# A second stream of forward transforms in a scan kernel, and later stores and loads around it

## The chip, the cores and the metric

The kernel runs on one core of one Trainium2 chip. The metric is the device time of one execution in microseconds (us); the time before is the median of three runs. Everything is computed in fp32.

## What is computed

Two layers, on an input of 4 images of 128 channels, 128 x 128 points each.

The first layer is a state-space scan. Each image is a sequence of 16384 tokens. Two small matrix products with a ReLU, then a projection to 256 channels of `x_in` and 256 of `z`; a causal convolution of 4 taps and a SiLU make `u`. From `u` come `delta` (softplus) and, per token, 16-vectors B and C. For each of the 256 channels and 16 states

```
h = h * exp(delta * A) + delta * B * u        # scan over the tokens
y = sum over states of h * C                  # plus u * D, times silu(z)
```

A projection back to 128 channels, a group norm over the image, a SiLU and the residual follow; the result is called x1.

The second layer filters x1 in the frequency domain. Four weights for each image come from a softmax over pooled, normed and projected channels. With X the two-dimensional real Fourier transform of x1 and four fixed filters, the product reduces to X times X times the weighted sum of the filters; it is transformed back, and half of x1 is added.

## The kernel before

**First block (`block0`).** It goes over 128 chunks of 512 tokens, 32 chunks an image, one image after the other. A chunk is cut into 16 slots, a slot being two scans of 128 partitions (32 channels by 4 states) by 512 tokens. All work is put into lists `todo[slot, phase]`, and a loop at the end of `block0` issues slot after slot, and in a slot phase after phase, in an order written out by hand:

```
for phase in ("turn", "sums", "pe", "exps", "late", "act", "pool", "dbu", "early", "gate", "scans", "dve", "end"):
```

A phase is a place in this order and not an engine. So each engine's queue has a fixed order, and what it waits for it gets from semaphores.

What a slot needs: ACT makes the decays (`da`, L469, `exps`). The products of delta, u and B come from POOL (`dbu`, L439) for three of each four scans; for the fourth PE transposes a tile `bt` (`dbu_turn`, L459) into the PSUM bank `b0`, of which there is one. DVE scans (L488). The product with C is made by DVE (L490) for some scans and by POOL (L495) for the others, and ACT keeps the last column as the next chunk's start (L491, L636). PE adds up the states in the bank `y` (`sums`, L505 for the term with D, L509), and DVE gates the result (`gate`, L519). A chunk has two halves of channels, and `y` has one bank: the sums of the second half, from slot 11 on, wait for the gate of the first half in slot 10.

Beside this, `pre(k)` prepares chunk k while chunk k-1 is scanned. `du_pool` (L340) multiplies delta by u on POOL, `du_turn(h)` (L320) transposes half of it on PE into a bank `pt`, and `bt_act` (L336) copies it on ACT, scaled, into the tile `bt`, eight pieces for each half. Before, the pieces of the first half stand in slots 8 to 11, `du_turn(1)` in slot 12 and the pieces of the second half in slots 12 to 14, in every chunk.

While image b+1 is scanned, image b is finished (`finish`): its group norm is applied in the chunks for which `norming(k)` holds (the third to the eighteenth of each later image; load L710 and L711, SiLU on ACT, addition on DVE, store of x1), and then come aggregation products (`agg`) for the pooling. From the 53rd chunk on, one stream of forward transforms is woven in (`spectrum`): three, three or two channels of x1 a chunk are loaded (slot 4), transformed over the height (slot 12, `over_h` L559, copied by ACT at L563) and over the width (slot 13, `over_w` L573, copied by ACT at L577), and stored to DRAM as `spec`. Three such pieces make a group of 8 channels. With EARLY = 2 the groups of image 0 and nine of image 1 are transformed there: 25 of 64.

**Second block (`block1`).** It goes over 64 units; a unit is 8 channels of one image, in three steps of 3, 3 and 2 channels. A unit whose spectrum is ready loads it (`sx`); the others transform x1 on PE (`over_h` L955 into `pa`, copied to `sa`; `over_w` L974 into `px`). All then take squares and products (ACT, DVE), sums (POOL), and the transform back (PE L1012, L1013, L1024; DVE L1018, and L1031 for the residual), and store `out`. The filters of a group are weighted on ACT (L922) and added on POOL (L932). Filter tiles `ft` come by DMA and serve several units. Image 3 is finished in the first units, its norm in steps 9 to 57 (two chunks in three steps, added by DVE at L724) and its aggregation after that, in steps 70 to 102, one chunk a step. So image 3 comes last; the images of the units, in order, with e where the spectrum is ready and F where it is made here, are, before:

```
0e 2F 1F  x7   0e 2F 1e  x6   3F 3F 3F
0e 3F 2F 3F 1e 3F 3F   0e 3F 2F 3F 1e 3F 3F   0e 3F 2F 3F 1e 3F 3F 3F
```

Units are counted from 0. All loads and stores of both blocks are issued on SP's queue, in the order of the program.

Of the kernel before, what the change touches and what calls it, by code (L numbers as in the profile page):

```python
# [26 lines left out]
F32 = mybir.dt.float32  # L27
# [7 lines left out]
T = 512  # L35
DG = 32
SQ = 4
NP = 16
CC = 8
EARLY = 2  # L40
KEEP = 4
LAG = 7
EPS = 1e-5
# [125 lines left out]
def block0(tc, s):  # L169
# [4 lines left out]
    with ExitStack() as ctx:  # L174
# [27 lines left out]
        def pre(k):  # L202
# [167 lines left out]
            if k == 0:  # L370
# [20 lines left out]
                    (NP, "pe", z_mm), (NP, "act", z_act), (NP + 3, "act", z_silu),  # L391
                ]
            late = k == 1
            return [
                (-14 - 10 * late, "pe", load), (-7 - 13 * late, "pe", h1_mm), (-6 - 13 * late, "act", h1_act),
                (-5 - 6 * late, "pe", xm_mm), (-4 - 6 * late, "act", xm_act),
# [7 lines left out]
                (9, "act", partial(bt_act, 0, 1, 3)),  # L404
                (10, "act", partial(bt_act, 0, 3, 5)), (11, "act", partial(bt_act, 0, 5, 8)),
                (12, "pe", partial(du_turn, 1)), (12, "act", partial(bt_act, 1, 0, 3)),
                (13, "act", partial(bt_act, 1, 3, 6)), (14, "act", partial(bt_act, 1, 6, 8)),
                (16, "pe", partial(rep_load, 1)),
            ]

# [102 lines left out]
        def post(k):  # L513

            b, i = divmod(k, NCH)
            d = st[k]

            def gate(j):
                nc.vector.tensor_mul(d["zs"][:, j, :], d["zs"][:, j, :], d["y", j])  # L519
# [22 lines left out]
            return [  # L542
                (26, "dve", partial(gate, 0)), (34, "dve", partial(gate, 1)), (36, "pe", o_mm), (37, "act", o_act),
                (49, "act", o_square),
                (50, "dve", done),
            ]

        def spectrum(b, c0, n):

            g = {}  # L550

            def load():
                g["x"] = p1.tile([s.H, 3, s.W], F32, tag="fx", name=f"fx_{b}_{c0}")
                nc.sync.dma_start(out=g["x"][:, 0:n], in_=s.x1[b][c0 : c0 + n].rearrange("c h w -> h c w"))

            def over_h():
                g["pa"] = psp.tile([s.W, 3, 2 * s.WF], F32, tag="pp", name=f"pp_fa_{b}_{c0}")
                for q in range(n):
                    nc.tensor.matmul(g["pa"][:, q], g["x"][:, q], s.fh, start=True, stop=True)  # L559

            def evict():
                g["sa"] = p1.tile([s.W, 3, 2 * s.WF], F32, tag="fs", name=f"fs_{b}_{c0}")
                nc.scalar.copy(g["sa"][:, 0:n], g["pa"][:, 0:n])  # L563

            def over_w():
                half = s.H // 2
                g["px"] = psp.tile([s.H, 3, 2 * s.WF], F32, tag="pp", name=f"pp_fx_{b}_{c0}")
                for q in range(n):
                    re, im = g["sa"][:, q, 0 : s.WF], g["sa"][:, q, s.WF :]
                    for (data, a, b_), start in (((re, s.fwr, s.fwr), True), ((im, s.fwi, s.fwm), False)):  # L570
                        for at, w in ((0, a), (1, b_)):
                            o = g["px"][at * half : (at + 1) * half, q]
                            nc.tensor.matmul(o, data[:, at : at + half], w, start=start, stop=not start)  # L573

            def store():
                x = p1.tile([s.H, 3, 2, s.WF], F32, tag="fq", name=f"fq_{b}_{c0}")
                nc.scalar.copy(x[:, 0:n].rearrange("h c r k -> h c (r k)"), g["px"][:, 0:n])  # L577
                nc.sync.dma_start(out=s.spec[b][:, c0 : c0 + n], in_=x[:, 0:n])

            return [  # L580
                (4, "pe", load), (12, "pe", over_h), (12, "end", evict), (13, "pe", over_w), (13, "end", store),
            ]
# [27 lines left out]
        chunk = NCH + NCH // 2 + 4  # L610
        for b in range(EARLY):
            for c0 in reversed(range(0, C, CC)):
                chunk = max(chunk, (b + 1) * NCH + NCH // 2 + 4)
                if chunk + 3 > n_chunks:
                    break
                for at, n in ((0, 3), (3, 3), (6, 2)):
                    for slot, phase, f in spectrum(b, c0 + at, n):
                        todo[slot + chunk * NP, phase].append(f)
                    chunk += 1
# [12 lines left out]
        with tc.manual_schedule():  # L632
            for n in range(min(slots), max(slots) + 1):
                for phase in ("turn", "sums", "pe", "exps", "late", "act", "pool", "dbu", "early", "gate", "scans", "dve", "end"):
                    for f in todo[n, phase]:
                        f()  # L636

# [52 lines left out]
def finish(s, io, b, first, norm, agg, add="dve", sums=True):  # L690
# [27 lines left out]
    def norm_dve(i):  # L718
        o, n = g["o", i], g.pop(("n", i))
        if sums:  # L720
            total = g["stat"][:, 0, i : i + 1]
            nc.vector.tensor_tensor_reduce(o, n, g["x", i], 1.0, 0.0, ALU.add, ALU.add, total)
        else:
            nc.vector.tensor_add(o, n, g.pop(("x", i)))  # L724
        nc.sync.dma_start(out=s.x1flat[b][:, i * T : (i + 1) * T], in_=o)

    def norm_stats(i):
        o = g.pop(("o", i))
# [84 lines left out]
def block1(tc, s):  # L813
# [10 lines left out]
    with ExitStack() as ctx:  # L824
# [76 lines left out]
        def load(n):  # L901
            if n < N:
# [124 lines left out]
        def residual(e, n, m, k):  # L1027
            if m == 0:
                u[n].ot = p2.tile([H, CC, W], F32, tag="ot", name=f"ot_{n}")
            o, xt = u[n].ot[:, m : m + k], u[n].xt[:, m : m + k]  # L1030
            nc.vector.scalar_tensor_tensor(o, xt, s.resw[0:H], e.po[:, 0:k], ALU.mult, ALU.add)  # L1031
            if m + k == CC:
                c0, b = units[n]
                nc.sync.dma_start(out=s.out[b, :, c0 : c0 + CC], in_=u[n].ot)

        with tc.manual_schedule():
            load(0)
            load(1)
            for t in range(3 * N + LAG + 3):
# [114 lines left out]
```

## Time and profile before

| | us |
|---|---|
| median of 3 runs | 7047.36 (7046.41 to 7050.6) |
| the profiled execution, its own time | 7042.62 |
| its span | 7040.8 |
| DVE busy | 6840.5 (97%) |
| POOL busy | 6802.5 (97%) |
| ACT busy | 6167.2 (88%) |
| PE busy | 5615.9 (80%) |

The span is the time from the first instruction to the last, as the profiler saw it. An engine's busy time is the sum of its instructions; the share of the whole span is a mean over stages with different limits, so the windows by stage say more. "Granted clock" is the share of its full speed at which PE was let run. A wait is named by the engine that ended it.

### The profile page before, as it was taken

How to read it: one execution, taken by the hardware profiler on the slowest of the kernel's cores; microseconds unless marked ns; L12 is line 12 of the kernel's file. 1: busy time of each engine (PE TensorE's matmuls, PEld its weight loads, DVE VectorE, ACT ScalarE, POOL GpSimd, SP SyncE). 2: the span in 40 equal slices, each digit the busy share in tenths (PEclk: the TensorE clock that was granted, in tenths of full speed). 3: DMA queues.
4: the chain of work that ended last, by engine and by line, in shares of the span. 5: the costliest groups of instructions: out<-in, count | busy, mean ns of one | idle time of the engine just before them, and what ended most of it. 6: DMA issues, size and time to landing. Idle time of an engine off the chain costs nothing. (4 is left out here: it accounts for less than half of the span.)

```text
span 7040.8 us, 95517 instructions
## 1 busy us (share of the span) xinstructions
PE 5615.9 (80%) x28742; PEld 2685.4 (38%) x28742; DVE 6840.5 (97%) x7914; ACT 6167.2 (88%) x13839; POOL 6802.5 (97%) x3010
## 2 busy tenths in 40 slices
PE   7777777777777788888777787887777787878999
PEld 3333333333333333333333333333333333327888
DVE  8999999999999999999999999999999999998877
ACT  7888888888888888889999988899999999888886
POOL 8999999999999999999999999999999999998887
PEclk9999989988998989999999999999999999999999
DMA  6676666766777777777877777777777877767865
GB/s 157 150 164 159 153 162 154 164 158 163 194 182 187 191 168 175 175 181 170 200 191 193 197 173 177 175 183 170 198 193 190 203 173 178 169 174 281 271 218 191
DMA packets 758088, 1285.91 MB, mean 183 GB/s; under 512 B 81584, under 2 KB 192704, under 8 KB 757568
## 3 DMA queue, kind: packets, MB, share of 16 engines
q1 hardware_dynamic: 757280, 1279.27, 73.2%
q8 instruction: 226, 3.70, 0.2%
q14 instruction: 294, 2.41, 0.1%
q10 hardware_dynamic: 288, 0.52, 0.0%
HBM read 1023.43 MB, written 256.06 MB: 182 GB/s over the span
## 5 line engine op out<-in xcount | busy, mean ns | idle before, releaser
L439 POOL TENSOR_TENSOR hb<-rdu,rB 128x512 f32<-128x512 f32 (+2 forms) x1537 | 3614.3, 2370 | 62.4 <-ACT rdu L360 32.9
L469 ACT ACTIVATE da<-rdelta,amat 128x512 f32<-128x512 f32 x4096 | 2804.4, 703 | 103.2 <-DVE h L488 98.7
L488 DVE TENSOR_TENSOR_SCAN da<-da,st,hb 128x512 f32<-128x512 f32 x2000 | 2446.9, 1266 | 25.3 <-ACT da L469 24.7
L495 POOL TENSOR_TENSOR hb<-h,rC 128x1024 f32<-128x1024 f32 (+1 forms) x1048 | 2411.9, 2303 | 55.0 <-DVE h L488 45.0
L490 DVE TENSOR_TENSOR hb<-da,rC 128x512 f32<-128x512 f32 x2064 | 1308.8, 673 | 2.2
L488 DVE TENSOR_TENSOR_SCAN h<-da,st,b 128x512 f32<-128x512 f32 x992 | 1257.6, 1268 | 2.7 <-PE b L459 2.7
L509 PE MATMUL y<-hb,sel 128*32 128x512 f32 x8192 | 1233.6, 675 | 12.9 <-POOL hb L495 12.5
L488 DVE TENSOR_TENSOR_SCAN h<-da,st,hb 128x512 f32<-128x512 f32 x976 | 1222.6, 1255 | 2.8 <-POOL hb L495 2.1
L459 PE MATMUL b<-ident,bt 128*128 128x128 f32 x4096 | 712.7, 295 | 487.2 <-DVE h L488 426.0
L255 PE MATMUL pp_cv<-xm,wck 128*128 128x512 f32 x2048 | 989.4, 627 | 3.0 <-ACT zs L249 2.6
L336 ACT ACTIVATE bt<-dut,xdt 128x256 f32<-128x256 f32 x2040 | 845.3, 483 | 114.7 <-PE dut L320 113.6
L459 PEld LDWEIGHTS b<-ident,bt 128*128 128x128 f32 x4096 | 516.3, 149 | 948.8 <-DVE h L488 708.3
L491 ACT COPY st<-da 128x1 f32<-128x1 f32 x2064 | 288.1, 163 | 454.6 <-DVE hb L490 450.5
L255 PEld LDWEIGHTS pp_cv<-xm,wck 128*128 128x128 f32 x2048 | 387.9, 199 | 632.5 <-issue 456.7
L320 PE MATMUL dut<-ident,du 128*128 128x128 f32 x1024 | 199.0, 328 | 475.4 <-POOL du L340 450.3
L932 POOL TENSOR_TENSOR wb<-wb,term 128x1040 f32<-128x1040 f32 x166 | 398.9, 2404 | 52.5 <-ACT term L922 47.0
L505 PE MATMUL y<-u,diag 128*128 128x512 f32 x512 | 307.1, 684 | 166.2 <-DVE zs L519 165.4
L320 PEld LDWEIGHTS dut<-ident,du 128*128 128x128 f32 x1024 | 141.9, 165 | 651.6 <-POOL du L340 582.0
L469 ACT ACT_TABLE_LOAD x261 | 334.9, 1283 | 4.6
L509 PEld LDWEIGHTS y<-hb,sel 128*32 128x32 f32 x8192 | 169.8, 113 | 374.5 <-issue 241.3
L294 PE MATMUL pp_dt<-xd,wdt 128*128 128x256 f32 x1024 | 286.8, 405 | 25.7 <-ACT xd L275 8.8
L244 PE MATMUL pp_z<-xm,win 128*128 128x512 f32 x512 | 274.8, 634 | 39.0 <-ACT fq L577 37.0
(197 smaller groups left out, 8376.9 us busy)
## 6 DMA issues: line engine op xcount, KB each, us to landing
rdelta<-dd SPq DMA_DIRECT2D x1020, 256.0 KB, 4.9
rdu<-dd SPq DMA_DIRECT2D x1020, 256.0 KB, 7.9
rC<-bc SPq DMA_DIRECT2D x512, 256.0 KB, 7.1
rB<-bc SPq DMA_DIRECT2D x512, 192.0 KB, 4.4
dd<-delta SPq DMA_DIRECT2D x255, 256.0 KB, 7.6
dd<-du SPq DMA_DIRECT2D x127, 512.0 KB, 6.6
ft<-in_filt_w SPq DMA_DIRECT2D x108, 520.0 KB, 6.4
xr<-in_x SPq DMA_DIRECT2D x128, 256.0 KB, 2.8
```

What stands on the lines that cost most here:

```text
L255: nc.tensor.matmul(ps["cv", j], w, d["xm"][:, t : t + T], start=t == 0, stop=t == KC - 1)
L320: nc.tensor.transpose(ps["dut", h][:, 2 * t + j, :], d["du"][:, j, at : at + P], s.ident)
L336: nc.scalar.activation(o, src, AF.Copy, scale=scale)
L439: nc.gpsimd.tensor_tensor(hb[:, p : p + n, :], d["du", j][:, m : m + n, :], d["B"][:, p - 1 : p - 1 + n, :], ALU.mult)
L459: nc.tensor.transpose(b[:, t * P : (t + 1) * P], src, s.ident)
L469: nc.scalar.activation(da, d["delta", j][:, m, :], AF.Exp, scale=s.amat[:, c : c + 1])
L488: nc.vector.tensor_tensor_scan(o, das[q], b, init, ALU.mult, ALU.add)
L490: nc.vector.tensor_tensor(hb[:, p + q, :], das[q], d["C"][:, p + q, :], ALU.mult)
L495: nc.gpsimd.tensor_tensor(hb[:, ps, :], h[:, q, :], d["C"][:, ps, :], ALU.mult)
L505: nc.tensor.matmul(y, s.diag[:, j, :], d["u"][:, j, :], start=True, stop=False)
L509: nc.tensor.matmul(y[m * DG : (m + 1) * DG, :], s.sel, d["hb", j, r][:, p, :], start=False, stop=r == NG - 1)
L932: nc.gpsimd.tensor_tensor(wb, wb, u[n].terms[f], ALU.add)
```

## The change

It has seven parts.

1. EARLY is 3, and `spectrum` has a second stream. A group's three pieces go each to the stream that is free earlier, so a group takes one and a half chunks instead of three. The second stream has its own tiles (`fy`, two buffers) and uses the PSUM bank `b0` of `dbu_turn`; its steps stand at the end of slots 14 (over the height) and 26 (over the width, which is slot 10 of the next chunk). The groups of images 0 and 1 and seven of image 2 are transformed in the first block: 39 of 64. Of the 117 pieces, 58 are on the second stream.
2. Both streams keep one tile for input, half transform and spectrum, instead of three.
3. The transposes for slots 0 and 12 come after the slot's sums on PE (the phase `late turn`), not before them.
4. In chunks that are not norming, `du_turn(1)` is in slot 11 instead of 12, and the `bt` pieces are placed earlier.
5. In chunks that are not norming, the gate of the first half stands ahead of the scans of slot 10 and not behind them.
6. The store of x1 in the norm (`norm_store`) is issued a slot later than the addition (a step later in the second block), and so is the store of `out` in the second block.
7. In the second block, spectra have three buffers instead of two, and filter loads that are not needed within three units are issued at the end of a unit's third step.

The units of the second block become

```
0e 2F 1e  x9   0e 2e 1e  x4   3F 3F 3F
0e 3F 2e 3F 1e 3F 3F   0e 3F 2e 3F 1e 3F 3F   0e 3F 2e 3F 1e 3F 3F 3F
```

The core of the diff:

```diff
-EARLY = 2
+EARLY = 3
...
+            if norming(k - 1):
+                pieces = [
+                    (9, "act", partial(bt_act, 0, 1, 3)), (10, "act", partial(bt_act, 0, 3, 5)),
+                    (11, "act", partial(bt_act, 0, 5, 8)), (12, "pe", partial(du_turn, 1)),
+                    (12, "act", partial(bt_act, 1, 0, 3)), (13, "act", partial(bt_act, 1, 3, 6)),
+                    (14, "act", partial(bt_act, 1, 6, 8)),
+                ]
+            else:
+                pieces = [
+                    (9, "act", partial(bt_act, 0, 1, 5)), (10, "act", partial(bt_act, 0, 5, 8)),
+                    (11, "pe", partial(du_turn, 1)), (11, "pool", partial(bt_act, 1, 0, 1)),
+                    (12, "act", partial(bt_act, 1, 1, 2)), (13, "act", partial(bt_act, 1, 2, 5)),
+                    (14, "act", partial(bt_act, 1, 5, 8)),
+                ]
...
-                (26, "dve", partial(gate, 0)), (34, "dve", partial(gate, 1)), ...
+                (26, "dve" if norming(k) else "gate", partial(gate, 0)), (34, "dve", partial(gate, 1)), ...
...
+            def bank(name, rows):
+                pool, to = (psd, "b0") if second else (psp, "pp")
+                return pool.tile([rows, 3, 2 * s.WF], F32, tag=to, name=f"{to}_{name}_{tag}")
...
             def evict():
-                g["sa"] = p1.tile([s.W, 3, 2 * s.WF], F32, tag="fs", name=f"fs_{b}_{c0}")
-                nc.scalar.copy(g["sa"][:, 0:n], g["pa"][:, 0:n])
+                nc.scalar.copy(g["f"][:, 0:n], g["pa"][:, 0:n])
...
+            if second:
+                return [
+                    (4, "pe", load), (14, "end", over_h), (14, "end", evict), (26, "end", over_w), (26, "end", store),
+                ]
             return [
                 (4, "pe", load), (12, "pe", over_h), (12, "end", evict), (13, "pe", over_w), (13, "end", store),
             ]
...
-            todo[n - 1, "turn"].append(partial(dbu_turn, n))
+            todo[n - 1, "turn" if n % NP not in (0, 12) else "late turn"].append(partial(dbu_turn, n))
...
-        nc.sync.dma_start(out=s.x1flat[b][:, i * T : (i + 1) * T], in_=o)
+
+    def norm_store(i):
+        nc.sync.dma_start(out=s.x1flat[b][:, i * T : (i + 1) * T], in_=g["o", i] if sums else g.pop(("o", i)))
...
+            (at[2] + 1, "end", partial(norm_store, i)),
...
-                    to, bufs = home(sum(e.early for e in u[:n]) % 2, 1, 2)
+                    to, bufs = home(sum(e.early for e in u[:n]) % 3, 1, 3)
...
                     for ft in loads[n]:
-                        load_filter(ft)
+                        if ft.first < n + 3:
+                            load_filter(ft)
...
+                    for ft in loads[n]:
+                        if ft.first >= n + 3:
+                            load_filter(ft)
...
+                store(t - LAG - 3)
```

More of the change, by code (lines that the diff above doesn't have):

```diff
@@ L403, in pre @@
                 (8 + late, "act" if late else "pool", partial(bt_act, 0, 0, 1)),
[L404 to L407, printed above, removed]
+                *pieces,
                 (16, "pe", partial(rep_load, 1)),
@@ L542, in post @@
             return [
-                (26, "dve", partial(gate, 0)), (34, "dve", partial(gate, 1)), (36, "pe", o_mm), (37, "act", o_act),
+                (26, "dve" if norming(k) else "gate", partial(gate, 0)), (34, "dve", partial(gate, 1)), (36, "pe", o_mm), (37, "act", o_act),
                 (49, "act", o_square),
@@ L546, in post, with spectrum @@
             ]
-        def spectrum(b, c0, n):
+        def spectrum(b, c0, n, second):
             g = {}
+            tag = f"{b}_{c0}"
+            def bank(name, rows):
+                pool, to = (psd, "b0") if second else (psp, "pp")
+                return pool.tile([rows, 3, 2 * s.WF], F32, tag=to, name=f"{to}_{name}_{tag}")
             def load():
-                g["x"] = p1.tile([s.H, 3, s.W], F32, tag="fx", name=f"fx_{b}_{c0}")
-                nc.sync.dma_start(out=g["x"][:, 0:n], in_=s.x1[b][c0 : c0 + n].rearrange("c h w -> h c w"))
+                pool, to = (p2, "fy") if second else (p1, "fx")
+                g["f"] = pool.tile([s.H, 3, 2 * s.WF], F32, tag=to, name=f"{to}_{tag}")
+                nc.sync.dma_start(
+                    out=g["f"][:, 0:n, 0 : s.W], in_=s.x1[b][c0 : c0 + n].rearrange("c h w -> h c w")
+                )
             def over_h():
-                g["pa"] = psp.tile([s.W, 3, 2 * s.WF], F32, tag="pp", name=f"pp_fa_{b}_{c0}")
+                g["pa"] = bank("fa", s.W)
                 for q in range(n):
-                    nc.tensor.matmul(g["pa"][:, q], g["x"][:, q], s.fh, start=True, stop=True)
+                    nc.tensor.matmul(g["pa"][:, q], g["f"][:, q, 0 : s.W], s.fh, start=True, stop=True)
             def evict():
-                g["sa"] = p1.tile([s.W, 3, 2 * s.WF], F32, tag="fs", name=f"fs_{b}_{c0}")
-                nc.scalar.copy(g["sa"][:, 0:n], g["pa"][:, 0:n])
+                nc.scalar.copy(g["f"][:, 0:n], g["pa"][:, 0:n])
             def over_w():
                 half = s.H // 2
-                g["px"] = psp.tile([s.H, 3, 2 * s.WF], F32, tag="pp", name=f"pp_fx_{b}_{c0}")
+                g["px"] = bank("fx", s.H)
                 for q in range(n):
-                    re, im = g["sa"][:, q, 0 : s.WF], g["sa"][:, q, s.WF :]
+                    re, im = g["f"][:, q, 0 : s.WF], g["f"][:, q, s.WF :]
                     for (data, a, b_), start in (((re, s.fwr, s.fwr), True), ((im, s.fwi, s.fwm), False)):
@@ L575, in store @@
             def store():
-                x = p1.tile([s.H, 3, 2, s.WF], F32, tag="fq", name=f"fq_{b}_{c0}")
-                nc.scalar.copy(x[:, 0:n].rearrange("h c r k -> h c (r k)"), g["px"][:, 0:n])
+                nc.scalar.copy(g["f"][:, 0:n], g["px"][:, 0:n])
+                x = g["f"].rearrange("h c (r k) -> h c r k", r=2)
                 nc.sync.dma_start(out=s.spec[b][:, c0 : c0 + n], in_=x[:, 0:n])
+            if second:
+                return [
+                    (4, "pe", load), (14, "end", over_h), (14, "end", evict), (26, "end", over_w), (26, "end", store),
+                ]
             return [
@@ L609, in block0 @@
                 todo[at + (b + 1) * NCH * NP, phase].append(f)
-        chunk = NCH + NCH // 2 + 4
+        free = [0, 0]
         for b in range(EARLY):
+            free = [max(c, (b + 1) * NCH + NCH // 2 + 4) for c in free]
             for c0 in reversed(range(0, C, CC)):
-                chunk = max(chunk, (b + 1) * NCH + NCH // 2 + 4)
-                if chunk + 3 > n_chunks:
+                steps, now = [], list(free)
+                for at, n in ((0, 3), (3, 3), (6, 2)):
+                    q = now.index(min(now))
+                    steps += [(slot + now[q] * NP, phase, f) for slot, phase, f in spectrum(b, c0 + at, n, q == 1)]
+                    now[q] += 1
+                if max(slot for slot, _, _ in steps) >= n_chunks * NP:
                     break
[L616 to L619, printed above, removed]
+                free = now
+                for slot, phase, f in steps:
+                    todo[slot, phase].append(f)
                 s.spectra.add((c0, b))
@@ L633, in block0 @@
             for n in range(min(slots), max(slots) + 1):
-                for phase in ("turn", "sums", "pe", "exps", "late", "act", "pool", "dbu", "early", "gate", "scans", "dve", "end"):
+                for phase in ("turn", "sums", "late turn", "pe", "exps", "late", "act", "pool", "dbu", "early", "gate", "scans", "dve", "end"):
                     for f in todo[n, phase]:
@@ L724, in norm_dve @@
             nc.vector.tensor_add(o, n, g.pop(("x", i)))
-        nc.sync.dma_start(out=s.x1flat[b][:, i * T : (i + 1) * T], in_=o)
+    def norm_store(i):
+        nc.sync.dma_start(out=s.x1flat[b][:, i * T : (i + 1) * T], in_=g["o", i] if sums else g.pop(("o", i)))
     def norm_stats(i):
-        o = g.pop(("o", i))
+        o = g.pop(("o", i)) if sums else g["o", i]
         if sums:
@@ L1031, in residual, with store @@
             nc.vector.scalar_tensor_tensor(o, xt, s.resw[0:H], e.po[:, 0:k], ALU.mult, ALU.add)
+        @block
+        def store(e, n, m, k):
             if m + k == CC:
@@ L1038, in block1 @@
             load(1)
-            for t in range(3 * N + LAG + 3):
+            for t in range(3 * N + LAG + 4):
                 n, i = divmod(t, 3)
```

## The prediction

> **What bounds the kernel now.** I read the page first, then windows by stage, then the vector engine's groups, then the timeline of one chunk.
>
> ```profile
> PE 5615.9 (80%) x28742; PEld 2685.4 (38%) x28742; DVE 6840.5 (97%) x7914; ACT 6167.2 (88%) x13839; POOL 6802.5 (97%) x3010
> ...
> DVE  8999999999999999999999999999999999998877
> ```
>
> The last slices differ from the rest, so I cut the span: the first block (31.4 to 6345) and three stages of the second.
>
> ```profile
> 31.40:6345.00 6313.60, 4949.55 (x22404) 2093.62 (x22402) 6267.20 (x6636) 5592.11 (x12635) 6219.23 (x2712) 0.93 0.74 176
> 6345.00:6420.50 75.50, 57.83 (x546) 52.42 (x547) 54.17 (x117) 64.98 (x131) 62.44 (x31) 0.86 0.70 250
> 6420.50:6550.00 129.50, 118.36 (x1216) 109.04 (x1215) 125.86 (x268) 112.07 (x225) 110.62 (x57) 1.00 0.92 323
> 6550.00:7040.80 490.80, 464.23 (x4512) 418.15 (x4510) 384.06 (x866) 381.31 (x822) 410.06 (x208) 0.99 0.66 220
> ```
>
> Columns: window, length, busy PE, PEld, DVE, ACT, POOL, then PE clock, DMA share, GB/s. The first block is DVE's: 6267 of 6314, 46 idle. A DVE stall there is lost time, and nothing done on PE or ACT costs anything until DVE waits for it. In the second block the middle stage is DVE's (125.9 of 129.5), and the last 491 us are mostly PE's (464). The change takes PE work out of the last stage and puts it, with ACT copies, into the first block.
>
> Where DVE waits from 2500 on, by its groups:
>
> ```profile
> L488 DVE TENSOR_TENSOR_SCAN da<-da,st,hb 128x512 f32<-128x512 f32 x1219 | 1491.6, 1266 | 23.8 <-ACT da L469 23.2
> ```
>
> The timeline puts 12 of the 23.2 us into ten plain chunks with transforms (0.8 to 1.5 each, slot 15) and 11 into the turns between batches. Chunk 56 shows why:
>
> ```profile
> 2823.98 1.20 ACT L336 ACTIVATE bt<-dut,xdt 128x256 f32<-128x256 f32 x3 [2.55 <-PE dut L320]
> ...
> 2829.77 2.47 DVE L488 TENSOR_TENSOR_SCAN da<-da,st,hb 128x512 f32<-128x512 f32 x2 [1.47 <-ACT da L469]
> ```
>
> ACT sits 2.55 us waiting for PE's `dut` and is late six us later. PE is late itself:
>
> ```profile
> 2810.92 1.98 PE L217 MATMUL pp_h<-xt,w 128*128 128x512 f32 x4
> 2814.79 0.66 PE L459 MATMUL b<-ident,bt 128*128 128x128 f32 x4 [1.88 <-DVE h L488]
> 2816.54 2.08 PE L505 MATMUL y<-u,diag 128*128 128x512 f32 x2 [1.10 <-DVE zs L519]
> 2818.55 1.94 PE L509 MATMUL y<-hb,sel 128*32 128x512 f32 x8
> 2820.41 3.10 PE L230 MATMUL pp_xm<-h,w 128*128 128x512 f32 x4
> 2823.34 0.60 PE L320 MATMUL dut<-ident,du 128*128 128x128 f32 x4
> ```
>
> It waits for the scan that frees bank b0, then for the gate (L519), and then runs at half clock:
>
> ```profile
> 2812.45:2815.86 3.41, 1.11 (x6) 0.42 (x4) 3.41 (x5) 3.41 (x11) 3.41 (x3) 1.00 0.94 330
> 2815.86:2819.27 3.41, 2.73 (x6) 0.71 (x10) 3.41 (x5) 3.41 (x9) 3.41 (x2) 0.50 1.03 245
> ```
>
> **Second block: 14 more groups arrive as spectra (39 loads of `sx` for 25; 200 matmuls into `pa` for 312).** A unit is 8 channels of one image. Windows of whole units, e with a spectrum, F without:
>
> ```profile
> 6550.37:6582.26 31.89, 29.10 (x304) 26.95 (x304) 26.29 (x58) 25.37 (x56) 27.05 (x15) 1.00 0.66 223
> 6582.26:6610.45 28.19, 25.91 (x231) 22.68 (x230) 23.84 (x57) 26.24 (x56) 27.10 (x15) 1.00 0.87 291
> 6642.65:6674.85 32.20, 30.71 (x244) 24.67 (x244) 24.25 (x56) 28.69 (x66) 27.65 (x15) 1.00 0.84 273
> 6798.95:6841.03 42.08, 40.92 (x435) 38.05 (x434) 33.11 (x74) 32.05 (x68) 35.91 (x19) 1.00 0.63 215
> ```
>
> They are e F F, e F e, e F e with aggregation, and e F F F. With e F F at 30.34 (6913.95 to 6944.29), F costs 42.08-30.34 = 11.7 and e 6.9 where PE is the bound: 4.8 an exchange. The exchanges:
> - Units 2, 5, 8, 11, 14 and 17 lie in the DVE stage: 0, but 1 at the start, where DVE has room.
> - Unit 20 turns e F F into e F e: 31.9-28.2 = 3.7.
> - Units 28 and 31 make e e e with aggregation. PE falls to some 26, so POOL (27.65) or DMA is next: 273 GB/s x 32.2 us and 0.53 MB more is 9.3 MB, at 273/0.84 = 325 GB/s 28.7 us. I take 29: 3.2 each, 6.4.
> - Units 34 and 37: 1.5 and 1.8, POOL and ACT being close behind.
> - Units 44, 51 and 58 stand between F's; e F is 18.6 of PE against 18.0 of POOL: 4.4 each, 13.2.
>
> Sum 27.6, between 16 (DMA or POOL next to all) and 34. The DVE stage gets 0.53 MB more for each three units; 323 GB/s at a share of 0.92 rises to some 340 of 351, still under DVE, with little to spare. The later stores take SP's wait for L724 (89 us in that stage) off the queue ahead of the loads behind it: DVE has only 3.6 us idle there, so 0 to 3; I take 0. In return a load into that buffer (L711) now waits for a store issued a step later, and the `out` stores, `xt` and filter loads queue behind it on SP: 0 to 5; I take 0, the load being due three steps on. The filter loads by two steps and the third `sx` buffer: 0, prefetched units ahead.
>
> **First block, DVE's waits for ACT.** With the gate ahead of slot 10's scans in plain chunks (those not norming), the sums start at the gate's end, not 3 us later, and `du_turn(1)` a slot earlier ends by my count below 2.5 us sooner, ACT's idle 2.55. `bt` pieces move from slots 11 and 12 to 9 and 10, where ACT leads by 1 us and more. The 12 us go; one ACT copy (0.5) more in slots 10 and 14 fits into that 2.55. Gain 12 (6 to 13). POOL gets slot 10's `h` 0.66 later, but starts that product 2.1 us after the scan anyway. At the turns, `y` ends 0.3 to 1.7 us after slot 10 begins, 7.5 us over seven chunks, and the early gate waits for it; against it stand the 11 us there. I take a gain of 2 (-6 to 8).
>
> **First block, the second stream.** It uses bank b0: `over_h` and its copy between the transposes for slots 14 and 16, `over_w` and its copy between those for 10 and 12. Now PE's transposes for slot 12, which DVE needs, stand behind `over_w`, the diagonal and the sums. Plain chunk, from slot 10's start, T: gate 0.58, scan to 1.85, b0 free; `over_w` from 1.93 (24 matmuls, 1.48 at L573), diagonal 0.95, sums 1.0, transposes 0.6 (chunk 71, full clock): done at 5.96. DVE reaches slot 12 at 2819.96-2813.47 = 6.49. ACT's copy (0.5, from about 3.5) hides under diagonal and sums. It fits by 0.5, at full clock.
>
> But PE is idle from T-0.5 to T+1.93, 2.4 us. Windows of 3.41 us in which PE was busy under about 0.4 are followed by half clock here (1.11 of 3.41 is 0.32 above; almost none with more than 0.5 busy are). A window holds 2.0 idle us or more in 1.9 of 3.41 us of its phases: half the chunks. Half clock for one window costs 1.7 us: done at 7.6, a stall of 1.1, 0.6 with two images; 0.9 on average. 36 such chunks: 36 x 0.5 x 0.9 = 16 (3 to 36). The Trainium skill, "TensorE: Matmul & The Clock Gate", section "HAM oscillation — how this bites in real kernels", asks only for no PE idle over about 3.4 us; by that a 2.4 us gap is harmless, this term 0 and the sum 16 lower. The row at 0.32, without any such gap, speaks against it, and I go by the row.
>
> Norming chunks keep gate and pieces. Chunk 71 has `pp_h` to T+3.3, so `over_w` ends at 4.8, transposes at 7.3: 0.8 late; chunk 70, with POOL's `du` and so PE earlier, fits. A stall lets POOL catch up, so not each of the 22 pays: 4 (1 to 16). Slot 16: `over_h` 0.7 and the copy before transposes that have 2 us left: 0 (to 6). Loads and stores of the stream add 0.4 MB to 49 us at a DMA share of 0.8: 0. The store of x1 goes a slot later past the stream's loads on SP; those land in 8 us and are due eight slots, some 24 us, later: 0. Chunks before 51 have neither stream nor stalls: 0.
>
> **Sum.** -27.6 - 12 - 2 + 16 + 4 = -21.6. The profiled run took 7042.62 (span 7040.8); that gives 7021.0. The median of before is 4.7 above it: 7026. Measurement of this kernel tells some 0.2%, 14 us, from no change.
>
> **Rivals.**
> - No throttle at slot 12: -41.6 to -37.6, 7006 to 7010. For it: PE is busier all round. Against: the row at 0.32.
> - The second block moves to its next bound, DMA share near 1: half of 27.6 goes, leaving about -8, 7040. For: 0.84 to 0.92 now, with e e e adding. Against: 344 GB/s is reached in places (6400 to 6450).
> - Slower: b0 delays slot 12's transposes in every one of 58 two-stream chunks. Each us of mean stall costs 58; -41.6 is eaten at 0.72 and 14 us lost at 0.96. At half clock in all plain chunks and POOL's lag kept in the norming ones it is 1.1: +22, 7069. For: slack 0.5 on a chain of four steps. Against: windows' phases drift.
>
> **How the numbers follow.** Forecast 0.40, no throttle 0.20, next bound 0.27, slower 0.13. Faster 0.60, same 0.27, slower 0.13. Range 7004 to 7052: from just under the first rival, past the second, into a part of the third.
>
> **What would show it.** Right: `pa` in the second block a third rarer; e e e triples near 29 us and e F pairs near 18.6; no wait of L488 for ACT `da` in plain chunks; waits of the b0 scan (L488, `h<-da,st,b`) for PE of some 20 us, with clock 0.50 in the windows just before. Wrong: that wait above 50 us or near 0; the DVE stage of the second block longer than before; ACT late again in slots 13 to 15.

## The result, and the profile after

The changed kernel takes 7066.10 us (median of 8 runs, 7065.23 to 7077.36), the kernel before beside it 7047.64: a ratio of 1.0033, with a 95% interval of 1.0024 to 1.0042. It is slower, by 18.5 us between the medians; the prediction said 21 us faster, in a range that ended at 7052. Five of the eight runs lie at 7065 to 7067 and three at 7074.8 to 7077.4. The profiled one is 7077.36 (span 7075.6), of the upper group, so it stands 34.7 above the profiled run of before (7042.62), and the sums below go by these two profiles.

The page, engines and DVE's slices:

```profile
PE 5598.7 (79%) x28742; PEld 2701.2 (38%) x28742; DVE 6844.7 (97%) x7914; ACT 6180.4 (87%) x13881; POOL 6806.3 (96%) x3010
...
DVE  8999999999999999999999999999999999998887
```

DVE and POOL do the same instructions as before, and DVE's busy time grew by only 4.2 us; the rest of the 35 us is waits. Windows over the first block and three stages of the second (columns as in the prediction):

```profile
31.40:6389.00 6357.60, 4997.67 (x23520) 2169.70 (x23519) 6271.70 (x6633) 5623.14 (x12713) 6223.22 (x2712) 0.94 0.75 178
6389.00:6464.07 75.07, 47.24 (x391) 42.37 (x390) 54.34 (x120) 64.03 (x131) 62.73 (x32) 0.86 0.78 267
6464.07:6608.27 144.20, 106.95 (x898) 98.94 (x898) 126.45 (x269) 107.41 (x213) 110.90 (x57) 0.88 0.88 296
6608.27:7075.60 467.33, 421.71 (x3868) 378.25 (x3867) 382.94 (x865) 368.98 (x797) 409.28 (x207) 0.99 0.71 243
```

In the first block DVE is idle for 85.9 us, where it was 46.4. In the second, the last stage has become short (PE 422 us, not 464), but DVE's stage, the third line, holds 144.2 us with 126.5 of DVE work; before, 129.5 held 125.9.

To compare kernels I cut each profiled run at the end of DVE's last scan, as the timeline has it. Before: 6337.0 us up to there and 703.8 after it. After: 6384.9 and 690.7. So the first block lost 47.9 and the second gained 13.1.

The first block's loss is in one group. The pages' lines of DVE's scans, before (L488) and after (L499):

```profile
L488 DVE TENSOR_TENSOR_SCAN da<-da,st,hb 128x512 f32<-128x512 f32 x2000 | 2446.9, 1266 | 25.3 <-ACT da L469 24.7
L488 DVE TENSOR_TENSOR_SCAN h<-da,st,b 128x512 f32<-128x512 f32 x992 | 1257.6, 1268 | 2.7 <-PE b L459 2.7
...
L499 DVE TENSOR_TENSOR_SCAN da<-da,st,hb 128x512 f32<-128x512 f32 x2000 | 2451.0, 1271 | 11.8 <-ACT da L480 11.2
L499 DVE TENSOR_TENSOR_SCAN h<-da,st,b 128x512 f32<-128x512 f32 x992 | 1263.1, 1273 | 54.9 <-PE b L470 54.8
```

Waits for ACT's `da` are halved (25.3 before). The scan that reads bank b0 waits 54.9 us for PE's transposes (2.7 before). By chunk and slot, in the timeline: 17.2 us in slot 12 of 14 plain chunks, 23.1 in slot 12 of 18 norming chunks, 3.5 in slot 12 of the turns (chunks 1 and 18 of an image, just ahead of the norming chunks and just behind them), and 8.5 in slot 0 behind the turns 50, 82 and 114. The clock's records tell these chunks from the others: of the 58 chunks with over_w in b0, the 32 plain and norming ones that wait are those with half clock, for 0.3 us or more, between the scans of slots 10 and 12; of the other 26, only the turns 65 and 97 wait. Chunk 71 is a norming one; PE's timeline, with one of over_w's lines:

```profile
3567.05 1.12 PE L320 MATMUL dut<-ident,du 128*128 128x128 f32 x4 [6.69 <-POOL du L340]
3567.96 1.06 PE L470 MATMUL b<-ident,bt 128*128 128x128 f32 x4
3568.95 1.94 PE L520 MATMUL y<-hb,sel 128*32 128x512 f32 x8
3570.82 2.55 PE L217 MATMUL pp_h<-xt,w 128*128 128x512 f32 x4
3573.30 0.44 PE L593 MATMUL b_fx<-c_fwr,fy 128*64 128x130 f32 x4
...
3574.78 1.12 PE L516 MATMUL y<-u,diag 128*128 128x512 f32 x2
3575.84 1.07 PE L520 MATMUL y<-hb,sel 128*32 128x512 f32 x8
3576.83 0.66 PE L470 MATMUL b<-ident,bt 128*128 128x128 f32 x4
```

and DVE's scan of slot 12:

```profile
3577.53 1.28 DVE L499 TENSOR_TENSOR_SCAN h<-da,st,b 128x512 f32<-128x512 f32 x1 [1.66 <-PE b L470]
```

PE gets POOL's `du` late, runs the sums at half clock (1.94 for what takes 1.07 later), then pp_h, and only then over_w, diagonal, sums and the transposes that DVE waits for.

The second block's loss shows in SP's queue (waits: line, what ended them, us in total, times, longest). The first line is before's, where the store of x1 waited for DVE's addition:

```profile
SPq L725 <- DVE of L724: 88.9, 27, 19.9
...
SPq L739 <- DMA x<-of: 79.7, 20, 7.9
```

and in DVE's waits from 6496 to 6608 (before's DVE stage has none of this kind):

```profile
DVE ot L1062 <- DMA out<-ot: 14.0, 3, 5.6
```

The load of L739 (L711 before) waits for the x1 store that is now issued a step later. The `out` stores stand behind it on SP, DVE waits for an `ot` buffer that such a store has not yet read, 3.5 to 5.6 us, and three groups of three units take 36.05, 38.12 and 37.54 where the one ahead of them takes 32.49.

### The profile page after: what moved, and what is told of

The parts are those of the page before. It is cut to its first block, busy times and chain, and to the rows that moved or that the text cites. A ratio compares the mean times of both kernels' runs of the same rounds, so it can differ in the third digit from the quotient of the medians.

```text
span 7075.6 us, 95863 instructions
## 1 busy us (share of the span) xinstructions
PE 5598.7 (79%) x28742; PEld 2701.2 (38%) x28742; DVE 6844.7 (97%) x7914; ACT 6180.4 (87%) x13881; POOL 6806.3 (96%) x3010
## 5 line engine op out<-in xcount | busy, mean ns | idle before, releaser
L499 DVE TENSOR_TENSOR_SCAN da<-da,st,hb 128x512 f32<-128x512 f32 x2000 | 2451.0, 1271 | 11.8 <-ACT da L480 11.2
L499 DVE TENSOR_TENSOR_SCAN h<-da,st,b 128x512 f32<-128x512 f32 x992 | 1263.1, 1273 | 54.9 <-PE b L470 54.8
L499 DVE TENSOR_TENSOR_SCAN h<-da,st,hb 128x512 f32<-128x512 f32 x976 | 1227.4, 1260 | 2.1 <-ACT da L480 1.7
L294 PE MATMUL pp_dt<-xd,wdt 128*128 128x256 f32 x1024 | 287.2, 404 | 29.3 <-ACT xd L275 11.8
```

What stands on the lines that cost most here:

```text
L499: nc.vector.tensor_tensor_scan(o, das[q], b, init, ALU.mult, ALU.add)
```

## The experiments

All ratios are to the kernel before, run beside it on the same chip. The medians come from different chips, on which the kernel before took 7045.41 (e1 to e4), 7051.17 (e5 to e8) and 7046.22 (e9 to e12); across these groups the ratios are to be compared. "First" is the end of the last scan and "second" what follows, in the profiled run; "b0" is the idle time ahead of the scan that reads bank b0, from the page's groups.

| kernel | median us | ratio (95%) | first | second | b0 |
|---|---|---|---|---|---|
| before | 7047.64 | 1 | 6337.0 | 703.8 | 2.7 |
| after | 7066.10 | 1.0033 (1.0024 to 1.0042) | 6384.9 | 690.7 | 54.9 |
| e1_one_stream | 7054.64 | 1.0013 (1.0004 to 1.0023) | 6335.0 | 715.6 | 8.7 |
| e2_plain_only | 7057.38 | 1.0014 (1.0004 to 1.0023) | 6359.1 | 695.3 | 31.1 |
| e3_store_now | 7048.23 | 1.0003 (0.9994 to 1.0013) | 6373.1 | 676.6 | 47.1 |
| e4_no_late_turn | 7138.88 | 1.0128 (1.0112 to 1.0144) | 6443.8 | 689.7 | 11.7 |
| e5_changed_again | 7070.80 | 1.0030 (1.0018 to 1.0042) | 6380.7 | 691.1 | 49.4 |
| e6_late_where | 7052.21 | 1.0005 (0.9996 to 1.0014) | 6372.7 | 674.6 | 41.5 |
| e7_over_behind_sums | 7035.51 | 0.9981 (0.9972 to 0.9990) | 6357.3 | 680.6 | 25.8 |
| e8_both | 7029.63 | 0.9974 (0.9964 to 0.9984) | 6347.4 | 683.8 | 10.5 |
| e9_fill_gap | 7037.65 | 0.9989 (0.9979 to 0.9998) | 6360.2 | 678.9 | 32.4 |
| e10_h_early | 7035.57 | 0.9987 (0.9978 to 0.9996) | 6363.6 | 679.0 | 21.5 |
| e11_turn_old | 7013.31 | 0.9955 (0.9940 to 0.9970) | 6325.2 | 686.6 | 3.3 |
| e12_late_also | 7017.31 | 0.9959 (0.9945 to 0.9974) | 6331.0 | 683.5 | 10.5 |

**Without the second stream.**

```diff
-                    q = now.index(min(now))
+                    q = 0
```

> The changed kernel with all pieces of the forward transforms in the first stream (25 groups arrive as spectra, as before); the placement of du, bt and gate by kind of chunk, the transposes after the sums in slots 12 and 0, the later stores and filter loads and three sx buffers stay. Theory A (the second stream costs the first block some 45 us through bank b0, the placement gains 12 there and loses 4 to 8 at the turns): the first block ends some 40 to 45 us sooner than in the changed kernel, the b0 scan waits for PE 3 us instead of 55, the second block is as long as before or up to 12 longer: 7040 to 7055. Theory B (the new order of the pieces, the gate and the late transposes costs the first block its 48 us): the first block stays as long as in the changed kernel and the second loses its gain: 7080 or more.

Theory A, but for the scan that reads b0, which still waits 8.7 us and not 3: 6.7 of it lies behind the turns, where the late transposes stay. The first block is 2 us shorter than before's: the waits for ACT in plain chunks are gone, and the turns take most of that back. The second block is 11.8 longer than before's although it has the same 25 spectra: parts 6 and 7 together cost that by themselves. It arises in units 7 to 15, where DVE waits 8.7 us for `out` stores.

**The second stream in plain chunks only.**

```diff
+                    while 2 <= now[1] % NCH < 20:
+                        now[1] += 1
                     q = now.index(min(now))
```

> The changed kernel with the second stream kept out of chunks 2 to 19 of every image, so out of the norming chunks and the two behind them; the first stream fills the chunks that stood empty, and 38 groups instead of 39 arrive as spectra. Theory A (over_w behind pp_h delays the transposes for slot 12 in norming chunks, 1.16 us each, some 25 us of the 55 in all): 25 us less in the first block, 2 to 4 more in the second: 7042 to 7048 in place of 7066. Theory B (what counts is how much PE has to do in a batch, wherever it lies): the waits move to the plain chunks and the time stays at 7060 to 7070.

The first block gains 25.8, and the b0 scans have 0.9 us of waits left in norming chunks, so the price of these chunks is confirmed. The second block gives back 4.6, so the profiled run is 21.2 shorter. Between the medians it is only 8.7, since the profiled run of after lies 11.3 above its own median. The plain chunks of image 3 are 8 us longer than in the profile of after (801.1 for 793.2), part of what theory B named.

**The store of x1 at once.**

```diff
-            (at[2] + 1, "end", partial(norm_store, i)),
+            (at[2] + sums, "end", partial(norm_store, i)),
```

(`sums` is false in the second block.)

> The changed kernel with the store of x1 in the second block's norming issued at once, in the step of its addition, as before; the first block's is unchanged. Theory A (SP waits 78 us in the load of L739 for a store issued a step later, and the queue behind it makes the units of the vector engine's stage 3 to 6 us longer, in some executions): the wait of that load falls under 15 us, the second block is 675 to 682 us, and no run lies above 7068: 7060 to 7066. Theory B (the stage is longer because three more spectra per nine units, 0.53 MB each, crowd the DMA engines): the units 9, 12, 15 stay above 15 us in some runs and times of 7075 still occur.

The second block falls by 14.1 to 676.6, as theory A had it; 13.0 of that is there by the end of unit 16, in four steps at the units 7, 10, 13 and 16. SP's wait in that load did not fall under 15, though; it halved:

```profile
SPq L739 <- DMA x<-of: 42.1, 15, 7.4
```

and so a part of DVE's wait for `out` stores stays, in the same stage:

```profile
DVE ot L1062 <- DMA out<-ot: 5.0, 3, 2.3
```

Windows of the unit group ahead and of the three next ones in e3:

```profile
6452.22:6484.69 32.47, 25.92 (x226) 23.57 (x226) 31.54 (x67) 26.85 (x54) 27.70 (x15) 0.95 0.86 302
6484.69:6519.60 34.91, 28.02 (x226) 25.82 (x226) 31.91 (x67) 26.87 (x54) 27.64 (x15) 0.85 0.87 303
6519.60:6554.45 34.85, 25.59 (x226) 23.52 (x226) 31.62 (x67) 26.86 (x54) 27.78 (x15) 0.95 0.97 336
6554.45:6588.21 33.76, 25.58 (x226) 23.32 (x226) 31.61 (x67) 26.83 (x54) 27.74 (x15) 0.95 0.95 332
```

The excess over 32.47 is now 1.3 to 2.4 for three units, not 3.6 to 5.6. Four later profiles with the same second block (e6, e7, e9, e10) have it at 674.6 to 680.6, so 14.1 stands for 10 to 16. The store of `out`, which part 6 delays too, was not put back by itself; what it costs is not known. Against the rival: the DMA share, 0.86 to 0.89 in after's long groups, is higher here (up to 0.97), where the groups are shorter. The first block was 11.8 shorter than in the profile of after, which this edit does not touch; e5 shows how much of that is chance.

**The transposes for slots 12 and 0 first again.**

```diff
-            todo[n - 1, "turn" if n % NP not in (0, 12) else "late turn"].append(partial(dbu_turn, n))
+            todo[n - 1, "turn"].append(partial(dbu_turn, n))
```

> The changed kernel with the transposes for slots 12 and 0 ahead of the sums, as for all other slots. Theory A (slot 12's scan waits because its transposes stand behind over_w, the diagonal and the sums): the copy that frees the bank ends 0.8 us before the sums do in chunk 71 (3576.07 against 3576.83), so the scan's wait shrinks by 0.4 to 0.8 us per chunk, 20 to 35 us in 58 chunks: 7030 to 7046. Theory B (PE is idle while ACT copies, and what stands behind, the sums, du's turn and the gate, comes later; or ACT copies late): the wait goes to other slots, 7060 to 7100.

Theory B, at 73 us above after, well over its range. The b0 scan's wait does fall to 11.7. But PE now stands until ACT has emptied b0, with diagonal, sums and du's transposes behind it. PE in chunk 89:

```profile
4500.49 1.11 PE L470 MATMUL b<-ident,bt 128*128 128x128 f32 x4 [1.09 <-ACT fy L596]
4501.40 1.92 PE L516 MATMUL y<-u,diag 128*128 128x512 f32 x2
4503.24 1.94 PE L520 MATMUL y<-hb,sel 128*32 128x512 f32 x8
4505.11 0.66 PE L320 MATMUL dut<-ident,du 128*128 128x128 f32 x4
```

ACT waits 4.67 us for that `dut`, and DVE a slot later 2.77 for ACT's `da`. The group `da<-da,st,hb` waits 103.5 us in this kernel, 11.8 in after. So where the second stream is in these slots, the late transposes of part 3 cost less than transposes that go first.

**The changed kernel once more.**

> The changed kernel as it is, once more, beside the next three. Theory A (the two levels of its time, 7065 and 7075, come from the second block's load that waits for a store; the first block's waits hang on the phase of PE's clock windows and vary by some 10 us from run to run): 7055 to 7077, the first block 20 to 50 us longer than before's. Theory B (the change as a whole costs a fixed 18 to 20 us): 7064 to 7067 in every run.

7062.0 to 7075.5 in six runs, first block 6380.7 and second 691.1: theory A for the spread. The second block repeats within 0.4 us, though, and e3's levels differ too (7043 to 7057), so the store alone does not make the two groups of times; the first block differs by 4 to 12 us between this run, e3's and after's with the same order there (b0 49.4, 47.1 and 54.9). What sets them is not settled.

**Late transposes only where the second stream has the bank.**

```diff
-            todo[n - 1, "turn" if n % NP not in (0, 12) else "late turn"].append(partial(dbu_turn, n))
+            todo[n - 1, "late turn" if n % NP in (0, 12) and n // NP - 1 in double else "turn"].append(partial(dbu_turn, n))
```

(on e3; `double` holds the chunks with a piece of the second stream.)

> The kernel of e3_store_now with the transposes behind the sums only in slots where the second stream holds bank b0 (the slot 12 and the slot 0 that follow one of its pieces); elsewhere they go first again, as before. Theory A (at the turns 50, 82 and 114 the transposes for the next chunk's slot 0 stand behind sums that POOL has late, 2.82 us each in e3): these three waits go, 8 us: 7038 to 7042 where e3 gave 7048, and the turns' idle falls from 5.0 to 2.2. Theory B (POOL and ACT are late there anyway, the wait moves to slots 1 to 3): 7046 to 7050.

The slot 0 waits behind the turns fall from 8.4 to 2.6 us. PE behind turn 50 in e3, where the sums go first, and DVE's scan:

```profile
2538.08 0.58 PE L772 MATMUL pp_bv<-mean,weff 128*128 128x1 f32 x2 [6.60 <-ACT zs L249]
2538.60 1.93 PE L520 MATMUL y<-hb,sel 128*32 128x512 f32 x8
2540.46 1.12 PE L470 MATMUL b<-ident,bt 128*128 128x128 f32 x4
```

```profile
2541.62 1.28 DVE L499 TENSOR_TENSOR_SCAN h<-da,st,b 128x512 f32<-128x512 f32 x1 [2.82 <-PE b L470]
```

and DVE in e6:

```profile
2540.79 1.28 DVE L499 TENSOR_TENSOR_SCAN h<-da,st,b 128x512 f32<-128x512 f32 x1 [0.86 <-PE b L470]
```

It is not POOL that is late, as theory A said, but PE: it sits 6.6 us for ACT and then runs the sums at half clock. The idle time in the turns 50, 82 and 114 with slot 0 behind them falls from 5.0 to 5.2 us to 3.2, 3.0 and 4.2. But slot 2 of the chunks behind them now waits for PE's transposes, 2.5 us in all, where it did not in e3; with it the turns take 4.4, 3.3 and 5.2, only 2.3 less, so theory B is right in part. The whole gains nothing that can be told (ratios 1.0003 and 1.0005); the norming chunks were 2.4 longer, by chance or by this order, and e12 does not settle it.

**over_w behind the sums in plain chunks.**

```diff
-                    (4, "pe", load), (14, "end", over_h), (14, "end", evict), (26, "end", over_w), (26, "end", store),
+                    (4, "pe", load), (14, "end", over_h), (14, "end", evict),
+                    (27, "over", over_w) if behind else (26, "end", over_w), (27, "over", store) if behind else (26, "end", store),
...
-                for phase in ("turn", "sums", "late turn", ...
+                for phase in ("turn", "sums", "over", "late turn", ...
```

(on e6.)

> The kernel of e6_late_where with over_w and its copy behind the diagonal and the sums of slot 11 in plain chunks, still ahead of the transposes for slot 12; norming chunks as they were. Theory A (PE sits idle 2.4 us for the b0 scan, is then granted half clock and runs over_w, diagonal and sums late; with diagonal and sums in that gap PE is busy and everything ends before slot 12): no half clock in slots 10 and 11 of plain chunks, the b0 scan's wait there falls from some 22 us to under 5, 15 to 18 us less than e6: 7020 to 7028. Theory B (half clock does not come from that gap, or sums wait for POOL's product, so that over_w only starts later): the wait stays or grows, 7040 to 7060.

Theory A: the plain chunks' slot 12 waits go from 16.9 us to 1.1, the first block is 15.4 shorter. Half clock of 0.3 us or more between the scans of slots 10 and 12 is found, in the clock's records, in 15 of the 36 plain chunks with over_w in b0 in e6 (51.2 us in all) and in 3 here (5.1 us). Chunk 88 in e6, PE and the window from slot 10 to slot 12:

```profile
4410.10 1.98 PE L217 MATMUL pp_h<-xt,w 128*128 128x512 f32 x4
...
4416.60 2.08 PE L516 MATMUL y<-u,diag 128*128 128x512 f32 x2
4418.60 1.23 PE L520 MATMUL y<-hb,sel 128*32 128x512 f32 x8
4419.77 0.66 PE L470 MATMUL b<-ident,bt 128*128 128x128 f32 x4
```

```profile
4413.24:4420.46 7.22, 5.81 (x40) 3.04 (x41) 5.97 (x7) 5.21 (x13) 7.22 (x5) 0.76 0.95 213
```

and in e7:

```profile
4404.80 1.98 PE L217 MATMUL pp_h<-xt,w 128*128 128x512 f32 x4
4407.54 1.13 PE L516 MATMUL y<-u,diag 128*128 128x512 f32 x2 [0.75 <-DVE zs L530]
4408.59 1.07 PE L520 MATMUL y<-hb,sel 128*32 128x512 f32 x8
...
4411.98 0.66 PE L470 MATMUL b<-ident,bt 128*128 128x128 f32 x4 [0.84 <-ACT fy L596]
```

In e6 the diagonal takes 2.08 at a mean clock of 0.76 in the window, and slot 12 waits 1.25. In e7 it takes 1.13, and the transposes are done 0.7 us before slot 12's scan starts at 4413.30.

**Only the gap filled.**

```diff
-                for j in range(NH):
-                    ...
-                    nc.tensor.matmul(ps["h", j], ...
+                for _ in range(2 if k - 2 > 52 and not 2 <= (k - 2) % NCH < 21 else 1):
+                    for j in range(NH):
+                        nc.tensor.matmul(ps["h", j], ...
```

(on e6.)

> The kernel of e6_late_where with the four matmuls of pp_h issued a second time in the plain chunks that have over_w in bank b0 (same operands, same bank, the group started anew): 2 us of PE work in the 2.4 us in which PE waits for the b0 scan, and nothing else moved. Theory A (that gap gives half clock to the next window, and half clock, not the length of the chain, makes slot 12 wait): half clock in slots 10 and 11 of plain chunks falls from 16 of 35 chunks in e6 to 5 or fewer, the b0 scan's waits there from some 20 us to 6: 12 to 15 us less than e6 although PE does more, 7034 to 7042. Theory B (the chain over_w, diagonal, sums, transposes is too long by itself): the waits stay or grow with PE's extra 2 us, 7050 to 7075.

This separates the clock from the order: e9 issues 140 matmuls more than e6 and is 12.5 us shorter in the first block, at the same order. Of the 12.5, 6.7 are waits in plain chunks, which the edit touches; the rest is within what the first block differs by between profiles of one order. Half clock in slots 10 and 11 is left in 4 of 36 plain chunks, 6.2 us of 51.2. Chunk 88, the same window:

```profile
4406.28:4412.17 5.89, 5.04 (x45) 2.73 (x44) 5.89 (x7) 5.21 (x13) 5.89 (x4) 1.00 0.99 224
```

Theory A, though not in full: 9.7 us of slot 12 waits stay in plain chunks and around the images' ends. In two of them (89, 95) the half clock lies earlier, on pp_h itself, where twice the matmuls now take longer.

**Both: over_w behind the sums, and the second stream in plain chunks only.**

```diff
+                    while 1 <= now[1] % NCH < 20:
+                        now[1] += 1
                     q = now.index(min(now))
```

(on e7.)

> The kernel of e7_over_behind_sums with the second stream kept out of chunks 1 to 19 of every image; 37 groups arrive as spectra instead of 39. Theory A (in norming chunks each second-stream piece makes slot 12 wait, some 18 us in e3): the norming chunks are back to before's 49.36 each, 18 us less in the first block, 4 to 9 more in the second: 7008 to 7020. Theory B (what counts is PE's work in a batch): the waits turn up in the plain chunks, as in e2, and the time stays at e7's.

Between the theories: no b0 wait in norming chunks, the first block 9.9 shorter and the second 3.2 longer, 5.9 less between the medians. The norming chunks stay at 795 an image (790 in e2), by small waits for ACT's `da` and POOL; the turns 65, 82, 97 and 114 are still at 4.8 to 5.1 idle us, and slot 2 behind them adds up to 1.3.

**pp_h early in norming chunks.**

```diff
-                (..., (-7 - 13 * late, "pe", h1_mm), ...
+                (..., (-7 - 13 * late - 2 * norming(k - 2), "pe", h1_mm), ...
```

(on e7.)

> The kernel of e7_over_behind_sums with pp_h's matmuls two slots earlier in norming chunks, ahead of du's transposes for which PE waits 6.3 us there. Theory A (in norming chunks PE is late because it waits for POOL's du and pp_h, 2.0 to 2.5 us, still stands between that and over_w): PE does pp_h in that wait, over_w starts at the b0 scan's end, the waits of slot 12 in norming chunks fall from some 17 us to under 6: 10 to 15 us less than e7, 7020 to 7027. Theory B (the norming chunks' waits come from POOL's lag itself, or the early pp_h blocks PE for xt or a bank): 7034 to 7050.

A miss: a ratio of 0.9987 where e7 had 0.9981. The norming chunks' slot 12 waits fall from 13.5 to 9.2 only, those for ACT's `da` rise from 2.2 to 5.1, and half clock covers 100 us of slots 10 and 11 of 30 norming chunks, by the clock's records, where it was 51. The edit also moves pp_h in the norming chunks of image 1, which have no transforms, and there the waits for ACT's `da` went from none to 5.5 us and the norming chunks from 790.5 to 796.6. With pp_h out of the way PE is idle again ahead of over_w. In chunk 71 the window from slot 10 to slot 12:

```profile
3567.88:3574.61 6.73, 6.73 (x47) 3.29 (x48) 6.62 (x7) 6.66 (x18) 6.73 (x4) 0.75 0.99 282
```

**The turns as before, and then the late transposes everywhere else.**

```diff
-            if norming(k - 1):
+            if norming(k - 1) or (k - 1) % NCH in (1, 18):
...
-                (26, "dve" if norming(k) else "gate", partial(gate, 0)), ...
+                (26, "dve" if norming(k) or k % NCH in (1, 18) else "gate", partial(gate, 0)), ...
```

(on e8, with the second stream out of chunk 0 as well.) The second kernel, e12, is e11 with one more edit (`NCH` is 32, the chunks of an image):

```diff
-            todo[n - 1, "late turn" if n % NP in (0, 12) and n // NP - 1 in double else "turn"].append(partial(dbu_turn, n))
+            todo[n - 1, "late turn" if n % NP == 12 or n % NP == 0 and n // NP % NCH != 19 else "turn"].append(partial(dbu_turn, n))
```

> The kernel of e8_both with before's places for gate, du's transposes and bt in the turn chunks (1 and 18 of each image), and the second stream out of chunk 0 as well; 37 groups as there. Theory A (at a turn y is late, so the early gate waits 1.5 us for it, and over_w in chunk 65 and 97 makes slot 12 wait 2.3): the turns' idle falls from 4.9 to before's 2 to 3.3, 8 to 12 us in all: 7018 to 7024. Theory B (the turn's waits for ACT's da in slot 15 are as long with either order, and slot 14's come on top): within 4 us of e8, 7026 to 7033.

> The kernel of e11_turn_old with the transposes for slots 12 and 0 behind the sums in every chunk again, but for slot 0 behind the turns 50, 82 and 114. Theory A (in e8 the norming chunks wait some 4 us more per image than in e2, in which the transposes stood last everywhere): 6 to 9 us less than e11, norming chunks at 49.4 each: 7010 to 7018. Theory B (these waits come with the phase of the clock windows and have nothing to do with that order): within 4 us of e11.

e11 takes 7013.31, 0.9955 of before (0.9940 to 0.9970): faster than both kernels. The turns' idle from 50 on is 2.1 to 3.8, 9.2 us less in all (11.4 with slot 2 behind them). The norming chunks have 4.4 us less of small waits besides, and DVE's time outside of waits is 3.7 less, neither of which theory A had claimed. Of its page, the b0 scan:

```profile
L499 DVE TENSOR_TENSOR_SCAN h<-da,st,b 128x512 f32<-128x512 f32 x992 | 1268.1, 1278 | 3.3 <-PE b L470 3.1
```

Its first block is 11.8 shorter than before's: the second stream's waits are gone there, and what is left is about the gain on ACT's waits in plain chunks (12.7). The second block, with 37 spectra, is 17.2 shorter. e12 is 4 us longer, so e2's even norming chunks did not come from the late transposes.

## Why the prediction was wrong

The sum was -21.6 against the profiled run; the profiled runs differ by +34.7, which is 56.3 more. Three steps failed, and they make 46.7 of that: the norming chunks, the load behind the later store, and the turns.

- **Second block, 27.6 of gain: right in the sum.** With the store put back it is 703.8 - 676.6 = 27.2 (23 to 29 by the five profiles). It is made up otherwise: 4.3 at the start and some 29 behind unit 16, where 1 and 26.6 were forecast, less some 6 that units 7 to 16 stay longer, where 0 was.
- **The load behind the later x1 store, taken as 0 (0 to 5): wrong, 14.1** (690.7 - 676.6), and 11.8 in e1 together with part 7. The step that failed is "the load being due three steps on". The text had named the queue, load, then `out` stores, `xt` and filters behind it, but priced the load by its own due time. What was due is the `out` store behind it: DVE waits for the buffer that it frees, 14.0 us in three places and 2.2 in a fourth; e3 has 5.0 left and before none.
- **ACT's waits, 12 of gain: right.** 12.7 us in plain chunks before, none after.
- **The second stream in plain chunks, 16: right in size (17.2) and in cause.** The 2.4 us gap did bring half clock, and filling it (e9) took most of it away (chunk 88's window has a clock of 0.76 in e6 and 1.00 in e9). The Trainium skill, "TensorE: Matmul & The Clock Gate", section "HAM oscillation — how this bites in real kernels", asks only for no PE idle over about 3.4 us and would have made this term 0.
- **Norming chunks, 4 (1 to 16): wrong, 23.1.** "A stall lets POOL catch up, so not each of the 22 pays" failed: 18 pay, 1.3 us each, chunk 70 too, which was to fit. The 0.8 worked out from chunk 71 was at full clock, and the throttle that was charged to plain chunks was left out here, where PE waits longer for `du` (6.69 in chunk 71). The 18 that pay are those with half clock between the scans of slots 10 and 12; the four at full clock wait for nothing. No run took the half clock out of these chunks alone, and in e5 and e3, with the same order, 15 and 14 of them pay 19.0 and 16.9. Even 22 x 0.8, without the catching up, would have given 17.6.
- **Turns, a gain of 2 (-6 to 8): wrong, a loss of about 12.** DVE's waits in chunk 1, in the six turns from 33 on and in slots 0 to 2 behind them went from 17.4 to 28.9: those for ACT's `da` did not fall (11.8 and 11.9), POOL's and a norm's 2.7 went, the early gate's for `y` came (4.3), and the b0 scan's rose from 2.7 to 12.4 (8.5 in slot 0 behind 50, 82 and 114, 3.5 in slot 12). The early gate was priced; the late transposes of part 3 were not, for slot 0 behind turns, in which the second stream has no piece (with them first again, in e6, 8.4 there becomes 2.6, and 2.5 in slot 2). e11, with gate and pieces back and the stream out of 65 and 97, has 13.6 less there than e8.
- **Slot 16, over_h ahead of the transposes, 0: right.** The slot 0 waits above 0.5 us are the three behind turns, which carry no piece.

Of the 34.7, these terms measured make -27.2 + 14.1 - 12.7 + 17.2 + 23.1 + 11.5 = 26.0. Of the other 8.7, 5.1 is DVE's time outside of waits up to the last scan, 3.3 are other waits in norming chunks and 0.9 is the gate's wait for `y` in chunk 53; why DVE's instructions took longer stays open. Two of the signs of being wrong that the prediction named came: the b0 scan waits above 50 us, and the second block's DVE stage is longer than before.

The third rival came closest, 7069 for 7066.10, and that is chance: a stall in all two-stream chunks, 1.1 us each, was near the mark for norming chunks (18 x 1.3), but of the plain chunks only 14 of 36 waited, as in the forecast. What it charged too much there was made up by the second block's 14 and the turns' 12, which no rival held.

## What to carry to other kernels

An engine that is idle on the whole still sets the time when new work is put on it between a wait and something that the bound engine needs: place such work so that it fills the gap (behind what is ready in the gap), and not so that it begins when the gap ends. A load that waits for a store costs what stands behind it in its queue, so look for the buffer that the queued transfers free, not for the load's own due time. When an order is changed for the sake of one kind of chunk, price it in the other kinds too; here a switch by kind (plain, norming, turn), with the store put back, turned 18 us of loss into 33 of gain.

## What the runs showed of the hardware

Three things were unexpected. More PE work can be faster: 140 repeated matmuls (28882 for 28742) cut slot 12's waits in plain chunks from 16.9 to 9.7 us, because a gap of 2.4 us no longer drew half clock. The clock went with the busy share of a stretch: in the profile of before from 2000 to 6300 us, cut into the 3.41 us grid on which the clock's records change, all 103 stretches with PE busy for less than 0.4 were followed by half clock, 25 of 75 with 0.4 to 0.5, and 28 of 1085 with more. And the same program's first block waits differ from run to run: 54.9, 49.4 and 47.1 us of b0 waits in after, e5 and e3, whose orders there are the same, with times that spread over 12 to 14 us.
